# Edge rows of a 7x7 depthwise stage read out of the main operand's rows, which are reordered in DRAM

## The chip, the core and the metric

The kernel runs on one core of a Trainium2 chip. The metric is the device time of one execution in microseconds. Before the change it was 2787.28 us, the median of three runs (2781.11 to 2789.88). The profiled execution spans 2784.9 us.

## What is computed

Two layers on an image of 384 channels and 192 x 192 pixels, float32, each with a residual. The second layer is the one that the change touches: a group normalisation and a 7x7 depthwise convolution with symmetrised weights.

```python
def _L1_conv_ref(x, weight):
    w_sym = (weight + rot90(weight, 1) + rot90(weight, 2) + rot90(weight, 3)) * 0.25
    return conv(x, w_sym, stride 1, padding 3, groups=C)      # 384 x 1 x 7 x 7

# layer 0
x = x + _L0_conv_ref(_gn(x), ...)   # 1x1 to q, k, v; 2x2 max; 3x3 depthwise; channel attention; 1x1
# layer 1
x = x + _L1_conv_ref(_gn(x), L1_conv_weight)
```

## The kernel before, in words

**Three stages.** Up to about 1480 us the first layer's q and k are made and their channel attention is formed. From 1480 to about 2200 us v is made block by block, the attention is applied and projected, and the residual is added. A block is two rows of each of the six row tiles of 32 rows (`RB` = 2, `NT` = 6, `TR` = 32). From about 2210 us the 7x7 stage runs over 48 steps of eight channels (`CB` = 8).

**How the 7x7 convolution becomes matmuls.** An image row is split by column phase: `CP` = 4 phases, each with 48 columns. A partition of the operand holds one pair of row within the tile (32) and phase (4), 128 in all; its free dimension holds eight channels, six row tiles and 50 columns (`JP`, 48 and a column of padding on either side). One such run of a channel is `RUN` = 300 elements, so eight channels of a partition are 2,400 elements, or 9,600 bytes, in one piece. The operand is called `main`. A row of the output also needs rows of the tiles above and below and phases of neighbouring columns. `main` holds the 32 own rows; the three rows above and the three below lie in a second operand, `aux`, in 60 of its partitions: `HALO` = 3 rows times `NQ` = 10 column positions, from partition `TOP` = 32 and again from `BOT` = 64. The two partitions after each group of thirty hold constants: the partition `ONE` = 62 holds ones, the other three zeros. The first and last 32 partitions of `aux` are copies from `main`. For each channel there are three matmuls, two on `main` with the weights `w` and one on `aux` with the weights `h`.

**How the operands get there.** In the second stage the sums of each block stand in SBUF tiles `sx`. POOL's queue stores their rows into the DRAM buffer `sd` (L1117), whose 128 outer rows are ordered by phase, then row. For the six rows at a tile's edge it also stores them, ten column positions each and shifted by one tile, into the DRAM buffer `sh` (L1127), whose 64 outer rows are those of `aux`. The constants of `sh` are written early from a tile `z` (L629). The weights are spread out by POOL in the first stage into DRAM buffers `wt` and `wh` (`weights`, L570 to L612).

**A step of the 7x7 stage.** Before step n computes, ACT's queue issues the loads of step n+2: `w`, `h`, `main` (one transfer of 128 rows of 9,600 bytes from `sd`) and `aux` (one of 64 such rows from `sh`); all four kinds come from helpers whose transfers are recorded at line L1227. The loads of steps 0 and 1 are issued on SP's queue. There are three buffers of each. Then POOL adds the mean to the border columns of `main` and `aux` (`borders`), PE makes the sums, ACT and DVE scale them out of PSUM into `apart` (L1500, L1502), POOL gathers them into `res` (L1441), and SP's queue stores four pieces of the output per step (L1445). The order of nearly all of this is the written one: `keep` holds each instruction in the program's order on its engine. The DMA semaphores are dealt out by the framework, eight for the transfers of the SP and ACT queues, taken in turn; a transfer waits for the one that had its semaphore before.

Of the kernel before, what the change touches and what calls it, by code (L numbers as in the profile page):

```python
# [59 lines left out]
TR = 32  # L60
# [26 lines left out]
def conv_preact_d2(  # L87
# [24 lines left out]

    sd = dram.tile([CP * TR, C, RUN], F32, name="sd")

    sh = dram.tile([SHR, C, RUN], F32, name="sh")

    wt = dram.tile([P, C, 2 * P], F32, name="wt")
    wh = dram.tile([SHR, C, P], F32, name="wh")  # L120
# [442 lines left out]
    with ExitStack() as bx:  # L563
# [6 lines left out]
        def weights(kt, i0, i1):  # L570
# [30 lines left out]
            for i in range(i0, i1):  # L601
                if HALO <= i < HALO + TR:
                    continue
                f = i * NQ if i < HALO else BOT - TOP + (i - HALO - TR) * NQ
                nc.gpsimd.dma_start(
                    wh[f : f + NQ, cs].rearrange("f c n -> c f n"),
                    bass.AP(
                        g.tensor,
                        g.offset + (i - i0) * GQ * TR,
                        [g.ap[0], [TR, NQ], [1, P]],  # L610
                    ),
                )  # L612

        pieces = [
            (kt, i0, min(i0 + GR, TR + 2 * HALO))
# [3 lines left out]
        with tc.issue_after(loaded):  # L619
            for kt in range(KT):  # L620
                cs = slice(kt * P, (kt + 1) * P)
                for f in (ONE, BOT + HALO * NQ):
                    nc.sync.dma_start(
                        wh[f - TOP : f - TOP + 2, cs].rearrange("f c n -> c f n"),
                        z[:, RUN : RUN + 2 * P].rearrange("p (f n) -> p f n", f=2),
                    )
                    for k in range(2):
                        one = f + k == ONE
                        nc.sync.dma_start(  # L629
                            sh[f + k - TOP, cs], z[:, 0:RUN] if one else z[:, RUN : 2 * RUN]  # L630
                        )

# [389 lines left out]
                pin(nc.scalar.activation(gl[:, ct, h * H : (h + 1) * H], ps[:, 0:H], AF.Gelu))  # L1022
        return gl

    sdv = sd.rearrange("(v r) c n -> r c v n", v=CP)

    def dve_keep(ins):

# [33 lines left out]
    def residual(i, ot, y, xr, pin):  # L1062
# [43 lines left out]
                yield  # L1106
        cs = slice(ot * P, (ot + 1) * P)

        def rows_of(a, nv, shift):
            o = LEAD + a * RUN + shift  # L1110
            return bass.AP(
                flat.tensor, flat.offset + o, [flat.ap[0], [RB * RUN, nv], [1, RUN]]
            )

        for a in range(RB):
            r = b * RB + a
            nc.gpsimd.dma_start(sdv[r, cs], rows_of(a, CP, 0))  # L1117

            halos = []
            if r >= TR - HALO:  # L1120
                halos.append(((r - TR + HALO) * NQ, -JP))
            if r < HALO:
                halos.append((BOT - TOP + r * NQ, JP))
            for h, shift in halos:
                for q in range(0, NQ, CP):
                    nv = min(CP, NQ - q)
                    nc.gpsimd.dma_start(  # L1127
                        sh[h + q : h + q + nv, cs].rearrange("f c n -> c f n"),
                        rows_of(a, nv, shift + q // CP),
                    )  # L1130


    spare = [(NBC, ct, dy) for ct in range(KT) for dy in (1, 2)]
# [65 lines left out]
    with ExitStack() as ex_:  # L1199
# [51 lines left out]

        def load_main(n):
            main = mainbufs[n % len(mainbufs)]
            queue(n)(main.rearrange("p c t j -> p c (t j)"), sd[:, span(n)])
            return main

        def load_aux(n):
            aux = auxs[n % len(auxs)]
            queue(n)(aux.rearrange("p c t j -> p c (t j)")[TOP:REST], sh[:, span(n)])
            return aux  # L1260


# [13 lines left out]
        part = wide.tile([P, 4], F32, name="part")  # L1276
        for k, (base, q) in enumerate(((TOP, 0), (BOT, 0), (TOP, NQ - HALO), (BOT, NQ - HALO))):
            hits = ident[:, base : base + HALO * NQ].rearrange("p (h q) -> p h q", q=NQ)
            nc.vector.tensor_reduce(
                part[:, k : k + 1], hits[:, :, q : q + HALO], AX.XY, ALU.add  # L1280
            )
        nc.vector.tensor_tensor(mask[:, 3:4], part[:, 0:1], part[:, 1:2], ALU.add)
        nc.vector.tensor_tensor(mask[:, 4:5], part[:, 2:3], part[:, 3:4], ALU.add)

        mv1 = const.tile([P, KT, 2], F32, name="mv1")
        yt = const.tile([P, KT], F32, name="yt")
# [86 lines left out]
        offs = wide.tile([P, KT, P], F32, name="offs")  # L1373
        nc.vector.tensor_scalar_mul(offs[:, 0, :], ones, off1[:, 0:1])
        for n in ws:
            nc.sync.dma_start(ws[n][1][ONE : ONE + 1], offs[span(n), 0, :])
# [3 lines left out]
        nc.sync.dma_start(wh[ONE - TOP].rearrange("(t p) n -> p t n", p=P), offs)  # L1380

        def borders(n):

# [194 lines left out]
```

## Time and profile before

| what | value |
|---|---|
| median of three runs | 2787.28 us |
| span of the profiled execution | 2784.9 us |
| granted TensorE clock, mean | 0.985 |
| busy: PE, DVE, ACT, POOL | 2591.1, 2456.2, 1140.1, 746.7 us |
| bytes moved by DMA | 581.01 MB, 209 GB/s over the span |
| 7x7 stage, `main` loads of ACT's queue | 46, the first at 2213.3 us, the last at 2740.4 us |

The page cuts the span into 40 slices of some 70 us each; the 7x7 stage is the last eight of them. The row of DMA digits is the mean busy share of the core's 16 DMA engines in tenths, and GB/s is what they moved in the slice:

```profile
PE   0399999999999999999899969999999899999998
POOL 1024443100000000000111321010101478787876
DMA  9976766301010110110336997566674899999998
GB/s 381 402 252 217 249 213 228 130 34 68 35 68 35 40 62 35 68 35 0 120 103 238 340 362 231 192 230 219 203 246 151 324 343 366 372 375 372 372 374 264
```

A row such as `aux<-sh ACTq DMA_DIRECT2D x46, 600.0 KB, 10.7` in the table of DMA issues is destination and source, issuing queue, how many, the size of one, and the median time from issue to landing in us:

```profile
sd<-sx POOLq DMA_DIRECT2D x96, 600.0 KB, 10.1
out_dram<-res SPq DMA_DIRECT2D x192, 288.0 KB, 11.2
main<-sd ACTq DMA_DIRECT2D x46, 1200.0 KB, 6.7
w<-wt ACTq DMA_DIRECT2D x46, 1024.0 KB
aux<-sh ACTq DMA_DIRECT2D x46, 600.0 KB, 10.7
sh<-sx POOLq DMA_DIRECT2D x36, 600.0 KB, 16.2
h<-wh ACTq DMA_DIRECT2D x46, 256.0 KB, 3.9
sh<-sx POOLq DMA_DIRECT2D x18, 300.0 KB, 16.0
```

### The profile page before, as it was taken

How to read it: one execution, taken by the hardware profiler on the slowest of the kernel's cores; microseconds unless marked ns; L12 is line 12 of the kernel's file. 1: busy time of each engine (PE TensorE's matmuls, PEld its weight loads, DVE VectorE, ACT ScalarE, POOL GpSimd, SP SyncE). 2: the span in 40 equal slices, each digit the busy share in tenths (PEclk: the TensorE clock that was granted, in tenths of full speed). 3: DMA queues.
4: the chain of work that ended last, by engine and by line, in shares of the span. 5: the costliest groups of instructions: out<-in, count | busy, mean ns of one | idle time of the engine just before them, and what ended most of it. 6: DMA issues, size and time to landing. Idle time of an engine off the chain costs nothing. (4 is left out here: it accounts for less than half of the span.)

```text
span 2784.9 us, 25837 instructions
## 1 busy us (share of the span) xinstructions
PE 2591.1 (93%) x8365; PEld 1525.2 (55%) x8365; DVE 2456.2 (88%) x3527; ACT 1140.1 (41%) x2262; POOL 746.7 (27%) x885
## 2 busy tenths in 40 slices
PE   0399999999999999999899969999999899999998
PEld 0144444444444444444556646666666677777776
DVE  7989998989999999999789958999889789888886
ACT  0143423333343333433402312232323577777776
POOL 1024443100000000000111321010101478787876
PEclk9999999999999999999899989999999999999999
DMA  9976766301010110110336997566674899999998
GB/s 381 402 252 217 249 213 228 130 34 68 35 68 35 40 62 35 68 35 0 120 103 238 340 362 231 192 230 219 203 246 151 324 343 366 372 375 372 372 374 264
DMA packets 234039, 581.01 MB, mean 209 GB/s; under 512 B 16640, under 2 KB 165744, under 8 KB 217136
## 3 DMA queue, kind: packets, MB, share of 16 engines
q1 hardware_dynamic: 173408, 283.44, 29.0%
q0 software_dynamic: 37376, 148.85, 15.8%
q10 hardware_dynamic: 23120, 147.07, 14.1%
q8 instruction: 67, 1.10, 0.2%
q14 instruction: 68, 0.56, 0.1%
HBM read 370.93 MB, written 208.21 MB: 208 GB/s over the span
## 5 line engine op out<-in xcount | busy, mean ns | idle before, releaser
L663 PE MATMUL pq<-xq,wq 128*128 128x512 f32 x2268 | 1028.8, 597 | 5.4 <-DVE ring L673 4.7
L708 DVE SCALAR_TENSOR_TENSOR qk<-ring,wd,qk 128x384 f32<-128x384 f32 x1152 | 699.4, 616 | 59.5 <-ACT ring L695 32.1
L663 PEld LDWEIGHTS pq<-xq,wq 128*128 128x128 f32 x2268 | 408.7, 190 | 437.3 <-issue 364.0
L549 PE MATMUL pv<-xv,wq 128*128 128x384 f32 x1656 | 545.7, 490 | 26.0 <-DMA xv<-in_x_dram 21.7
L549 PEld LDWEIGHTS pv<-xv,wq 128*128 128x128 f32 x1656 | 316.7, 192 | 245.8 <-issue 20.4
L1482 PE MATMUL pc<-main,w 128*128 128x288 f32 x1536 | 436.4, 406 | 3.0 <-PE al L1515 1.7
L1502 DVE TENSOR_SCALAR apart<-pc,rb 32x576 f32<-32x576 f32 x384 | 312.1, 813 | 81.2 <-PE pc L1482 55.4
L1482 PEld LDWEIGHTS pc<-main,w 128*128 128x128 f32 x1536 | 290.6, 190 | 87.1 <-issue 2.4
L725 ACT COPY qkT<-turns 32x288 f32<-32x288 f32 x768 | 329.0, 428 | 20.7 <-DVE turns L791 9.3
L1500 ACT ACTIVATE apart<-pc,rb 32x576 f32<-32x576 f32 x384 | 281.1, 732 | 133.5 <-PE pc L1482 128.7
L959 DVE SCALAR_TENSOR_TENSOR vb<-rows,wd,vb 128x576 f32<-128x576 f32 x384 | 313.3, 817 | 11.3
L673 DVE TENSOR_REDUCE ring<-pq 128x128 f32<-128x512 f32 x428 | 292.1, 683 | 3.7 <-PE pq L663 3.6
L1482 PE MATMUL pc<-aux,h 128*128 128x288 f32 x768 | 248.1, 405 | 0.0
L719 ACT ACTIVATE junk<-qk 128x384 f32<-128x384 f32 x144 | 71.1, 494 | 411.8 <-DVE qk L708 411.0
L1441 POOL COPY res<-apart 128x1152 f32<-128x1152 f32 (+1 forms) x96 | 222.0, 2338 | 13.3 <-ACT apart L1500 9.5
L826 POOL TENSOR_TENSOR rn<-rn,halfpos 128x6 f32<-128x6 f32 x1 | 1.4, 1359 | 827.5 <-DVE rn L825 827.5
L1076 DVE TENSOR_TENSOR sx<-xr,y 128x576 f32<-128x576 f32 x180 | 203.8, 1173 | 19.9 <-ACT y L1047 14.8
L555 DVE TENSOR_REDUCE rows<-pv 128x192 f32<-128x768 f32 x144 | 137.7, 957 | 84.7 <-PE pv L549 84.6
L1117 POOL DMA_DIRECT2D sd<-sx x96 | 72.2, 755 | 514.5 <-DVE sx L1076 493.2
L741 PEld LDWEIGHTS grams<-qkT,qkT 128*96 128x96 f32 x576 | 92.8, 165 | 147.3 <-issue 136.1
L1096 ACT ACTIVATE wq<-sx,negmid 128x1152 f32<-128x1152 f32 x96 | 120.6, 1257 | 122.5 <-DVE sx L1076 118.2
L1482 PEld LDWEIGHTS pc<-aux,h 128*128 128x128 f32 x768 | 145.1, 189 | 41.2 <-issue 0.2
(227 smaller groups left out, 2270.6 us busy)
## 6 DMA issues: line engine op xcount, KB each, us to landing
sd<-sx POOLq DMA_DIRECT2D x96, 600.0 KB, 10.1
out_dram<-res SPq DMA_DIRECT2D x192, 288.0 KB, 11.2
main<-sd ACTq DMA_DIRECT2D x46, 1200.0 KB, 6.7
xv<-in_x_dram SPq DMA_DIRECT2D x138, 384.0 KB, 6.6
xr<-in_x_dram SPq DMA_DIRECT2D x45, 1152.0 KB, 11.7
xq<-in_x_dram SPq DMA_DIRECT2D x21, 2304.0 KB, 8.2
w<-wt ACTq DMA_DIRECT2D x46, 1024.0 KB
xs<-in_x_dram SPq DMA_DIRECT2D x24, 1536.0 KB, 15.1
```

The source lines that it names most:

```text
L549: nc.tensor.matmul(ps[:, u, 0 : RB * HW], wq[:, kt, o : o + P], xb[:, u, kt, :], start=(kt == 0), stop=(kt == KT - 1),)
L555: nc.vector.tensor_reduce(rows[ct][:, 1 + t0 : 1 + t0 + UT, 1 : PS + 1], ps[:, :, 0 : RB * HW].rearrange("p u (a w b) -> p u w a b", a=2, ...
L663: ins = nc.tensor.matmul(ps, wq[:, kt, ct * P : (ct + 1) * P], rows[:, kt, :, g * 64 : (g + 1) * 64], start=(kt == 0), stop=(kt == KT - 1) ...
L673: nc.vector.tensor_reduce(t[:, r0 : r0 + PR, 1 + g * 32 : 1 + (g + 1) * 32], ps.rearrange("p (h a w b) -> p h w a b", h=PR, a=2, b=2), AX. ...
L708: nc.vector.scalar_tensor_tensor(dst, src, w, dst, ALU.mult, ALU.add)
L725: nc.scalar.copy(side[f * Q : (f + 1) * Q].rearrange("p c (t n) -> p t c n", n=P)[:, :, :, a * Q : (a + 1) * Q], turns[a * Q : (a + 1) * Q ...
L959: pin(nc.vector.scalar_tensor_tensor(dst, src, w, dst, ALU.mult, ALU.add))
L1076: nc.vector.tensor_tensor(bass.AP(flat.tensor, flat.offset + at(e) + a * RUN, [flat.ap[0], [JP, NT], [1, NJ], [at(f) - at(e), 2]],), xq[:, ...
L1441: keep(copy(res[ps, k], apart[ps, :, k].rearrange("p e n -> p n e")))
L1482: nc.tensor.matmul(ahead[q][:, k, 0 : NT * NJ], lhs, rhs, start=(j == 0), stop=(j == 2), skip_group_check=True,)
L1500: keep(nc.scalar.mul(dst, src, scale))
L1502: keep(nc.vector.tensor_scalar_mul(dst, src, scale))
```

## The change

The buffer `sh` and its stores go: every edge row is already in `sd`, since a column position to the left or right of the four phases is a phase of the neighbouring column, one element on, and the tile above or below is `JP` elements before or after. `sd` is ordered by row, then phase, so that the four phases of three consecutive rows are twelve rows in a row. `aux` is loaded straight from `sd`, by two transfers for the rows above and two for the rows below: one for the first eight column positions (24 partitions) and one for the last two (6 partitions). They are issued on SP's queue. The order of the partitions within a group of thirty changes with that, and the weights `wh` and the masks follow it. The constants of `aux` are loaded once into each of the three buffers and stay there.

```diff
-    sd = dram.tile([CP * TR, C, RUN], F32, name="sd")
-    sh = dram.tile([SHR, C, RUN], F32, name="sh")
+    sd = dram.tile([TR * CP, C, RUN], F32, name="sd")
+    cst = dram.tile([3, P, RUN], F32, name="cst")
...
-                f = i * NQ if i < HALO else BOT - TOP + (i - HALO - TR) * NQ
-                nc.gpsimd.dma_start(
-                    wh[f : f + NQ, cs].rearrange("f c n -> c f n"),
...
+                base, h = (0, i) if i < HALO else (BOT - TOP, i - HALO - TR)
+                for q in range(0, NQ, CP):
+                    nq = min(CP, NQ - q)
+                    f = base + q * HALO + h * nq
+                    nc.gpsimd.dma_start(
+                        wh[f : f + nq, cs].rearrange("f c n -> c f n"),
...
-    sdv = sd.rearrange("(v r) c n -> r c v n", v=CP)
+    sdv = sd.rearrange("(r v) c n -> r c v n", v=CP)
...
         for a in range(RB):
-            r = b * RB + a
-            nc.gpsimd.dma_start(sdv[r, cs], rows_of(a, CP, 0))
-            halos = []
...
-            for h, shift in halos:
-                for q in range(0, NQ, CP):
-                    nv = min(CP, NQ - q)
-                    nc.gpsimd.dma_start(
-                        sh[h + q : h + q + nv, cs].rearrange("f c n -> c f n"),
-                        rows_of(a, nv, shift + q // CP),
-                    )
+            nc.gpsimd.dma_start(
+                sdv[b * RB + a, cs],
+                bass.AP(
+                    flat.tensor, flat.offset + LEAD + a * RUN,
+                    [flat.ap[0], [RB * RUN, CP], [1, RUN]],
+                ),
+            )
...
         def load_main(n):
             main = mainbufs[n % len(mainbufs)]
-            queue(n)(main.rearrange("p c t j -> p c (t j)"), sd[:, span(n)])
+            queue(n)(
+                main.rearrange("p c t j -> p c (t j)"),
+                bass.AP(
+                    sd.tensor, sd.offset + n * CB * RUN,
+                    [[C * RUN, CP], [CP * C * RUN, TR], [1, CB * RUN]],
+                ),
+            )
             return main
 
         def load_aux(n):
             aux = auxs[n % len(auxs)]
-            queue(n)(aux.rearrange("p c t j -> p c (t j)")[TOP:REST], sh[:, span(n)])
+            flat = aux.rearrange("p c t j -> p c (t j)")
+            for base, r, shift in ((TOP, TR - HALO, -JP), (BOT, 0, JP)):
+                for q in range(0, NQ, 2 * CP):
+                    nq = min(2 * CP, NQ - q)
+                    rows = [[1, 2], [C * RUN, HALO * CP]]
+                    if nq < 2 * CP:
+                        rows = [[CP * C * RUN, HALO], [C * RUN, nq]]
+                    rows = rows + [[1, CB * RUN]]
+                    keep(
+                        nc.sync.dma_start(
+                            flat[base + q * HALO : base + (q + nq) * HALO],
+                            bass.AP(
+                                sd.tensor,
+                                sd.offset + (r * CP * C + n * CB) * RUN + shift + q // CP,
+                                rows,
+                            ),
+                        )
+                    )
             return aux
+
+        def load_constants(aux):
+            flat = aux.rearrange("p c t j -> p c (t j)")
+            for p, k in ((ONE, 0), (BOT + HALO * NQ, 1)):
+                keep(nc.sync.dma_start(flat[p : p + 2], cst[k : k + 2, 0:CB]))
...
         hs = [load_h(n) for n in range(2)]
-        for n in range(2):
-            ws[n] = ws[n] if n == 0 else load_w(n), hs[n]
-            aux = load_aux(n)
-            mains[n] = load_main(n), aux
+        for aux in auxs[0:2]:
+            load_constants(aux)
+        mains[0] = load_main(0), load_aux(0)
+        ws[0], ws[1] = (ws[0], hs[0]), (load_w(1), hs[1])
+        main1 = load_main(1)
...
+        mains[1] = main1, load_aux(1)
+        load_constants(auxs[2])
```

In these access patterns a pair is a step in elements and a count, slowest first. Left out are the masks (`part` has six columns for six reductions where it had four), the early writes of the constants (three into `cst` where twelve went into `sh`), and `keep` around two small stores of offsets.

More of the change, by code (lines that the diff above doesn't have):

```diff
@@ L603, in weights @@
                     continue
-                f = i * NQ if i < HALO else BOT - TOP + (i - HALO - TR) * NQ
-                nc.gpsimd.dma_start(
-                    wh[f : f + NQ, cs].rearrange("f c n -> c f n"),
[L607 to L611, printed above, removed]
-                )
+                base, h = (0, i) if i < HALO else (BOT - TOP, i - HALO - TR)
[5 more added lines that the diff above has]
+                        bass.AP(
+                            g.tensor,
+                            g.offset + ((i - i0) * GQ + q) * TR,
+                            [g.ap[0], [TR, nq], [1, P]],
+                        ),
+                    )
         pieces = [
@@ L626, in conv_preact_d2 @@
                     )
[L627 to L631, printed above, removed]
+            for k in range(3):
+                nc.sync.dma_start(cst[k], z[:, 0:RUN] if k == 0 else z[:, RUN : 2 * RUN])
         ring = []
@@ L1107, in residual @@
         cs = slice(ot * P, (ot + 1) * P)
[L1109 to L1112, printed above, removed]
-            )
-        for a in range(RB):
-            r = b * RB + a
-            nc.gpsimd.dma_start(sdv[r, cs], rows_of(a, CP, 0))
-            halos = []
[L1120 to L1123, printed above, removed]
-            for h, shift in halos:
-                for q in range(0, NQ, CP):
-                    nv = min(CP, NQ - q)
-                    nc.gpsimd.dma_start(
-                        sh[h + q : h + q + nv, cs].rearrange("f c n -> c f n"),
-                        rows_of(a, nv, shift + q // CP),
-                    )
+        for a in range(RB):
+            nc.gpsimd.dma_start(
[4 more added lines that the diff above has]
+                ),
+            )
     spare = [(NBC, ct, dy) for ct in range(KT) for dy in (1, 2)]
@@ L1258, in load_aux @@
             aux = auxs[n % len(auxs)]
-            queue(n)(aux.rearrange("p c t j -> p c (t j)")[TOP:REST], sh[:, span(n)])
-            return aux
+            flat = aux.rearrange("p c t j -> p c (t j)")
[9 more added lines that the diff above has]
+                            flat[base + q * HALO : base + (q + nq) * HALO],
+                            bass.AP(
+                                sd.tensor,
+                                sd.offset + (r * CP * C + n * CB) * RUN + shift + q // CP,
+                                rows,
+                            ),
+                        )
+                    )
+            return aux
+        def load_constants(aux):
+            flat = aux.rearrange("p c t j -> p c (t j)")
+            for p, k in ((ONE, 0), (BOT + HALO * NQ, 1)):
+                keep(nc.sync.dma_start(flat[p : p + 2], cst[k : k + 2, 0:CB]))
         ws, mains = {0: load_w(0)}, {}
         hs = [load_h(n) for n in range(2)]
-        for n in range(2):
-            ws[n] = ws[n] if n == 0 else load_w(n), hs[n]
-            aux = load_aux(n)
-            mains[n] = load_main(n), aux
+        for aux in auxs[0:2]:
[3 more added lines that the diff above has]
+        main1 = load_main(1)
         mask = wide.tile([P, 5], F32, name="mask")
@@ L1275, in conv_preact_d2 @@
         nc.vector.memset(mask[0 : 2 * TR, 2:3], 1.0)
[L1276 to L1281, printed above, removed]
+        part = wide.tile([P, 6], F32, name="part")
+        for k, base in enumerate((TOP, BOT)):
+            for i, (q, nq, lo, hi) in enumerate(
+                ((0, CP, 0, HALO), (CP, CP, CP - 1, CP), (2 * CP, NQ - 2 * CP, 0, NQ - 2 * CP))
+            ):
+                o = base + q * HALO
+                hits = ident[:, o : o + nq * HALO].rearrange("p (h q) -> p h q", q=nq)
+                nc.vector.tensor_reduce(
+                    part[:, 2 * i + k : 2 * i + k + 1], hits[:, :, lo:hi], AX.XY, ALU.add
+                )
         nc.vector.tensor_tensor(mask[:, 3:4], part[:, 0:1], part[:, 1:2], ALU.add)
-        nc.vector.tensor_tensor(mask[:, 4:5], part[:, 2:3], part[:, 3:4], ALU.add)
+        nc.vector.tensor_reduce(mask[:, 4:5], part[:, 2:6], AX.X, ALU.add)
         mv1 = const.tile([P, KT, 2], F32, name="mv1")
@@ L1375, in conv_preact_d2 @@
         for n in ws:
-            nc.sync.dma_start(ws[n][1][ONE : ONE + 1], offs[span(n), 0, :])
+            keep(nc.sync.dma_start(ws[n][1][ONE : ONE + 1], offs[span(n), 0, :]))
         along(rb, rstd1, 0)()
@@ L1379, in conv_preact_d2 @@
             nc.vector.tensor_scalar_mul(offs[:, kt, :], ones, off1[:, kt : kt + 1])
-        nc.sync.dma_start(wh[ONE - TOP].rearrange("(t p) n -> p t n", p=P), offs)
+        keep(nc.sync.dma_start(wh[ONE - TOP].rearrange("(t p) n -> p t n", p=P), offs))
+        mains[1] = main1, load_aux(1)
+        load_constants(auxs[2])
         def borders(n):
```

## The prediction

> **What bounds the kernel now.** I read the table of stretches first, then the waits and the DMA table of the last stretch, because the diff changes how that stage is fed. Columns of the first fence: stretch, length, busy time of each engine, granted clock, DMA share, GB/s.
>
> ```profile
> 147.00:1480.00 1333.00, 1306.57 (x3618) 620.60 (x3617) 1218.27 (x2051) 478.04 (x1242) 171.55 (x258) 0.99 0.30 103
> 1480.00:2170.00 690.00, 658.82 (x2234) 427.80 (x2233) 599.53 (x688) 197.19 (x436) 104.63 (x140) 0.97 0.73 246
> 2170.00:2216.00 46.00, 36.63 (x145) 27.55 (x144) 29.55 (x59) 22.86 (x42) 21.59 (x34) 0.89 0.96 358
> 2400.00:2600.00 200.00, 200.00 (x826) 155.60 (x825) 172.19 (x173) 154.69 (x191) 157.52 (x155) 1.00 1.03 372
> ```
>
> Up to 2170 us PE sets the pace. In the 7x7 stage (from 2210) PE and the DMA engines are both full: share 1.03, 372 GB/s. The waits of 2216 to 2760 say which gives way:
>
> ```profile
> ACT apart L1500 <- PE pc L1482: 123.4, 47, 4.3
> POOL main L1390 <- DMA main<-sd: 78.1, 38, 3.8
> DVE apart L1502 <- PE pc L1482: 51.0, 32, 6.0
> ```
>
> The evictions wait for PE; POOL waits for `main` 38 times, 3.8 us at most. So loads arrive just in time: a transfer twice as long would stop the stage. The 45 intervals between the ACT queue's `main` loads (2213.3 to 2740.4) are 11.7 us each: that is a step. The DMA table of the same stretch gives what the rows cost:
>
> ```profile
> q10 hardware_dynamic: 20340, 143.36, 70.2%
> q1 hardware_dynamic: 72000, 53.10, 29.8%
> ```
>
> In the trace's single DMA records a 9,600-byte row (`main`, `aux`) takes 361 ns (median, 361 to 362 at the ninetieth percentile), an 8,192-byte row of `w` 309 ns, a 4,096-byte row of `h` 159 ns, a 768-byte row of `out` 36 ns. Spread over 16 engines, an engine's step is 8 rows of main (2.89 us) + 4 of aux (1.44) + 8 of w (2.47) + 4 of h (0.64) + 96 of out (3.46) = 10.9 us, against 11.7 measured. The ACT queue's share, 0.702 x 544 us = 382 us over 46.5 steps, is 8.2 us a step against 7.44 from the medians: rows of that queue took 10% more on average.
>
> [...] On the page the ACT queue has
>
> ```profile
> q10 hardware_dynamic: 23120, 147.07, 14.1%
> ```
>
> packets. Its transfers move 19,848 rows, which leaves 3,272; 205 transfers with 16 completions each would leave 3,280. Eight are missing, and just one transfer of that queue, the eight rows of `tmpr`, has fewer than 16 rows. [...]
>
> **The change, part by part.**
>
> 1. *Edge rows no longer stored.* The 54 stores `sh<-sx` (36 x 600 + 18 x 300 KB = 27.6 MB) go. At 372 GB/s these are 74 us of all engines, and they fall between 1489 and 1680, where the DMA share is 0.85 to 1.03. PE waits there:
>
> ```profile
> PE pv L549 <- DMA xv<-in_x_dram: 21.7, 3, 15.9
> ```
>
> Without these stores that stretch moves what the next one does (share 0.63 to 0.68, no such wait), so I count **-22 us**, -10 if half is another transfer's doing.
>
> 2. *54 stores of `wh` instead of 18*: 36 more issues on POOL at 0.95 us (`wh<-g`, L605), 34 us, mostly before 520 us, where POOL's digits on the page are 2 to 4 and it waits 189 us itself for `wt<-g` and `wh<-g`. No wait list of that stretch names POOL as a releaser that holds PE. 0. Six edge constants of 300 KB in all become three: 0. The six `part` reductions instead of four (0.15 us each on DVE) and the new order of SP's first loads: 0 and under 1 us.
>
> 3. *`sd` rows by (row, phase) instead of (phase, row).* The 96 stores have the same 512 rows of 1,200 bytes; only the step between them changes. 0. The load of `main` changes shape: the source is now 4 phases x 32 rows x 9,600 bytes, the destination 128 partitions. [...]32 rows on each of engines 0 to 3 instead of 8 on each of 16. 32 x 0.361 = **11.55 us** on those four.
>
> 4. *Edge rows of `aux` from `sd`, on SP.* 60 rows instead of 64, by two transfers with source 2 x 12 rows and destination 24 partitions ([...]12 rows each on engines 0 and 1) and two with source 3 x 2 and destination 6 ([...]2 rows each on 0 to 2). Engine 0: 2 x 12 + 2 x 2 = 28 rows, **10.1 us**, instead of 4 rows.
>
> Engine 0's step is then 11.55 + 10.1 + 2.47 + 0.64 + 3.46 = **28.2 us**, with eleven completions 28.4. If the rows of main, aux, w and h take the 10% more that the ACT queue's did, 30.9. [...] I take 29.5. PE's 48 matmuls, DVE's and POOL's work of a step fit in 11.7 us and lie beside it. The loads run up to two steps ahead into three buffers, so engine 0 has a queue; each interval grows by 29.5 - 11.7 = 17.8 us, and 47 intervals by **+837**.
>
> 5. *Start of the stage.* `main` of step 0 is issued at 2193.7 and POOL takes it at 2203.7. With 11.55 + 10.1 = 21.7 us on engine 0 and about 2 us of completion it is 2217: **+12**, since aux now queues beside it. The chain of the normalisation (to 2209) hides none of what lies beyond.
>
> 6. *A new wait.* In the changed program's order a step has 11 transfers on SP and ACT where it had 8, and each waits for the completion of the one eight places earlier: SP's second edge transfer waits for `main` of the step before, and behind it in SP's queue stand the other two and four stores; ACT's `main` load waits for a store of the step before, and behind it stand ACT's evictions, for which PE's sums wait. All of these are shorter than engine 0's own queue, so I price it at 0; at the most two completions a step are exposed, 2 x 2.8 us (the shortest landing of `out`).
>
> Sum: 2787 - 22 + 12 + 837 = **3614 us**.
>
> **The rivals.**
>
> - *All 16 engines work whatever the pattern* (faster). For: main and aux carry the same bytes in rows of the same 9,600 bytes, and POOL's transfers with mixed shapes fill all engines now. Against: those have 128 on both sides, and the missing eight completions show that row counts matter on the hardware queues. Aux is 4 rows fewer, the stage stays at PE's 11.7, part 1 remains: 2787 - 22 = 2765. Chance 0.09.
> - *The narrow transfers lie on different engines.* Main on four, aux on others: 11.55 + 2.47 + 0.64 + 3.46 = 18.1, with 5% 19.0; 47 x 7.3 = 343; 2787 - 22 + 6 + 343 = 3114. [...] Chance 0.06.
> - *Part 6 is exposed*: 29.5 + 5.6 = 35.1 a step; 47 x 23.4 = 1100; 3877. For: eight counters for eleven transfers, and SP already waits 198.9 us for earlier stores. Against: there are two queues, and a transfer of the other keeps engine 0 busy. Chance 0.13.
> - *Engine 0 bounds, near its own sum* (the forecast): 28.4 to 30.9, so 3562 to 3680. Chance 0.72.
>
> **How the numbers follow.** The time is the forecast's. Range: the forecast's bounds, with a gain of 10 instead of 22 and a start of up to 20 late above, and half-exposed completions (32.3 a step, 3746): 3530 to 3780. That leaves out the two cheap rivals (0.15) and the worse half of the third. Slower by over 0.3% are the last three cases, 0.91; faster 0.07; 0.02 within 0.3%, where all engines work and the gain of part 1 is made elsewhere.
>
> **What would show it.** Part 3 and 4: on the page after, the ACT queue has 23,120 - 46 x 80 (aux with completions) - 46 x 12 (completions of main) = 18,888 packets; 19,440 if main uses 16. The DMA digits of the last stage fall from 9 to about 4, PE's too, and 372 GB/s to some 150; POOL waits for `main` or `aux` some 18 us a step; `main` lands 12 us or more after issue, instead of 6.7. Part 1: no wait of PE for `xv` near 1640. Wrong, if the stage still takes 11.7 us a step: then the engine count doesn't follow the outer dimension. If the step is above 33 us with engine 0 not full, part 6 failed.

## The result, and the profile after

The changed kernel takes 3817.66 us, the median of four runs (3796.8 to 3841.02). The kernel before takes 2786.57 us, the median of four (2781.11 to 2789.88). The ratio is 1.3706, with a 95% interval of 1.3651 to 1.3761. The forecast was 3614 us, with a range up to 3780: the direction and the main mechanism were right, the size was too small by 204 us. The profiled executions span 2784.9 us before and 3825.3 us after; all stages below are compared in these two.

The slices of the page of after, PE's and the DMA engines' busy tenths and what was moved:

```profile
PE   0799999999999899999999643252352433523425
DMA  9766631111111044666665634444444444444444
GB/s 390 291 242 231 227 116 46 50 50 50 50 50 50 1 136 163 215 224 226 226 225 177 214 103 141 118 126 120 117 136 119 115 134 127 127 125 117 134 114 130
```

The 7x7 stage now fills seventeen slices of 96 us where it filled eight of 70. In it the DMA engines are busy four tenths of the time and move 103 to 141 GB/s; before it was nine tenths and 372. PE, full before, works two to five tenths. Nothing is full on average: a mean over sixteen engines can hide that a few of them have most of the work. In the single DMA records at most four rows of any kind are under way in 63% of the time (2400 to 3600).

The page's table of DMA queues, ACT's and SP's:

```profile
q1 hardware_dynamic: 175312, 308.59, 24.4%
q10 hardware_dynamic: 18888, 118.80, 11.0%
```

18,888 packets on ACT's queue is what the prediction worked out for a `main` load on four engines. Had it kept sixteen, there would be 46 x 12 = 552 more completions. The single DMA records agree: from 2400 to 3600 ACT's queue never has more than four rows of 9,600 bytes under way at once, but for 0.3% of the time; before, it had up to sixteen. SP's queue has no more than three under way but for 0.04% of the time, and both queues together no more than four but for 0.7%, which fits edge rows on engines that carry `main`; the records don't name engines.

Two stretches of after, columns as in the prediction's first fence:

```profile
1620.00:1690.00 70.00, 70.00 (x242) 45.79 (x241) 64.29 (x72) 22.39 (x50) 7.50 (x10) 1.00 0.60 197
2400.00:2600.00 200.00, 77.81 (x288) 58.58 (x288) 49.77 (x60) 53.99 (x66) 53.75 (x54) 0.69 0.45 122
```

And the first of them before:

```profile
1620.00:1690.00 70.00, 48.30 (x146) 28.98 (x145) 39.36 (x45) 11.42 (x25) 14.11 (x19) 0.80 0.94 321
```

From 1620 to 1690 PE had stood still for 22 us, waiting for `xv` under a DMA share of 0.94. After, it is full. The last addition into `sx` starts at 2162.0 us instead of 2194.9: a gain of 33 us by the end of that stage. From 2400 to 2600 PE is busy 78 of 200 us, where it was busy all 200.

The waits of 2400 to 3600 in after, first of the compute engines, then of SP's queue:

```profile
POOL aux L1437 <- DMA aux<-sd: 907.6, 54, 45.6
ACT apart L1527 <- PE pc L1509: 865.1, 34, 52.7
PE pc L1509 <- POOL aux L1444: 777.1, 18, 47.5
```

```profile
SPq L1265 <- DMA main<-sd: 344.3, 17, 21.8
SPq L1472 <- DMA aux<-sd: 219.2, 53, 11.2
SPq L1472 <- DMA w<-wt: 200.1, 17, 13.5
SPq L1472 <- DMA out_dram<-res: 125.9, 18, 9.0
```

Read from below: PE waits for POOL, POOL waits for the rows of `aux` to land. SP's queue, which issues these rows (L1265), is itself held 17 times until a `main` has landed: that is the wait for a semaphore which part 6 of the prediction named and priced at nothing. The instructions of `main` in after, ACT's loads alone (duration of the issue in ns as lowest, median and highest, then first and last start):

```profile
L1213 ACTq DMA_DIRECT2D main<-sd x46: 579/580/630, 2218.0 to 3753.5; - x46
```

(3753.5 - 2218.0) / 45 = **34.1 us** a step, against 11.7 before and 29.5 forecast. The account of the whole: 33 us earlier into the stage; the first of these loads 37.6 us later after the stage's beginning (4.7 us later on the clock); 45 intervals of 22.4 us more, 1008.4; and 27.3 us more after the last load. -32.9 + 37.6 + 1008.4 + 27.3 = 1040.4, the difference of the spans (it must come out, since the four are cut from the same two spans).

### The profile page after: what moved, and what is told of

It is laid out like the page before. It is cut to its first block, busy times and chain, and to the rows that moved or that the text cites. A ratio compares the mean times of both kernels' runs of the same rounds, so it can differ in the third digit from the quotient of the medians.

```text
span 3825.3 us, 26098 instructions
## 1 busy us (share of the span) xinstructions
PE 2651.4 (69%) x8365; PEld 1560.4 (41%) x8365; DVE 2367.0 (62%) x3529; ACT 1140.7 (30%) x2262; POOL 715.7 (19%) x867
## 3 DMA queue, kind: packets, MB, share of 16 engines
q1 hardware_dynamic: 175312, 308.59, 24.4%
q10 hardware_dynamic: 18888, 118.80, 11.0%
## 5 line engine op out<-in xcount | busy, mean ns | idle before, releaser
L1509 PE MATMUL pc<-aux,h 128*128 128x288 f32 x768 | 278.7, 448 | 987.7 <-POOL aux L1444 940.3
L1509 PEld LDWEIGHTS pc<-aux,h 128*128 128x128 f32 x768 | 157.0, 209 | 1045.2 <-POOL aux L1444 976.8
L1509 PE MATMUL pc<-main,w 128*128 128x288 f32 x1536 | 473.6, 434 | 19.5 <-POOL main L1417 13.1
L1509 PEld LDWEIGHTS pc<-main,w 128*128 128x128 f32 x1536 | 316.1, 206 | 118.4 <-POOL main L1417 16.5
L1437 POOL TENSOR_TENSOR aux<-aux,mm 32x96 f32<-32x96 f32 x96 | 41.9, 436 | 1139.2 <-DMA aux<-sd 1137.5
L1076 DVE TENSOR_TENSOR sx<-xr,y 128x576 f32<-128x576 f32 x180 | 203.9, 1174 | 19.4 <-ACT y L1047 15.2
L1468 POOL COPY res<-apart 128x1152 f32<-128x1152 f32 (+1 forms) x96 | 207.5, 2192 | 5.8 <-DVE apart L1529 3.0
```

What stands on the lines that cost most here:

```text
L1076: nc.vector.tensor_tensor(bass.AP(flat.tensor, flat.offset + at(e) + a * RUN, [flat.ap[0], [JP, NT], [1, NJ], [at(f) - at(e), 2]],), xq[:, ...
L1468: keep(copy(res[ps, k], apart[ps, :, k].rearrange("p e n -> p n e")))
L1509: nc.tensor.matmul(ahead[q][:, k, 0 : NT * NJ], lhs, rhs, start=(j == 0), stop=(j == 2), skip_group_check=True,)
```

## The experiments

All experiments are read by that step, and beside it stands the sum of the rows on engine 0. By that name the prediction has the engine with a share of every load; no record names one, so the sum is an estimate, from the counts of engines and the durations that the prediction took from the trace of before (9,600-byte row 361 ns, `w` 309, `h` 159, `out` 36). "Wide" is a load whose larger part lies on twelve or sixteen engines, "narrow" one on two to four. The four runs of the changed kernel differ by up to 44 us, which is 1 us a step; all experiments but two were run once, and several on different chips, so differences of a step under 1 us are not read.

| kernel | `main` | `aux` | transfers a step | rows of engine 0, us | step, us | excess |
|---|---|---|---|---|---|---|
| before | wide | wide | 8 | 10.9 | 11.7 | 0.8 |
| both_wide_eight | wide | wide | 8 | 10.9 | 11.9 | 1.0 |
| after_both_wide | wide | wide | 11 | 11.6 | 14.5 | 2.9 |
| after_main_wide | wide | narrow | 11 | 19.6 | 20.9 | 1.3 |
| main_four | narrow | wide | 8 | 19.6 | 26.4 | 6.8 |
| after_aux_wide | narrow | wide | 11 | 20.3 | 27.6 | 7.3 |
| main_four_aux_two | narrow | narrow | 8 | 29.7 | 32.2 | 2.5 |
| after | narrow | narrow | 11 | 28.2 | 34.1 | 5.9 |

### Is it the number of engines?

Only `main` narrow, in the kernel before (`sh` and its stores stay):

```diff
-    sdv = sd.rearrange("(v r) c n -> r c v n", v=CP)
+    sdv = sd.rearrange("(r v) c n -> r c v n", v=CP)
...
-            queue(n)(main.rearrange("p c t j -> p c (t j)"), sd[:, span(n)])
+            queue(n)(
+                main.rearrange("p c t j -> p c (t j)"),
+                bass.AP(sd.tensor, sd.offset + n * CB * RUN,
+                    [[C * RUN, CP], [CP * C * RUN, TR], [1, CB * RUN]]),
+            )
```

> The kernel before with one part of the change alone: rows of sd ordered by row and phase, and main loaded as 4 x 32 rows. sh, its stores and the single aux transfer stay, eight transfers a step. Theory N (narrow transfers: [...]the fullest engine's rows are the step): 11.55 + 1.44 + 2.47 + 0.64 + 3.46 = 19.6 us a step nominally, 20 to 21 measured, 3180 to 3230 us in all. Theory W (the new waits of eleven transfers made the step, width costs nothing): 11.7 us a step, 2787 us. Theory H (a narrow transfer also holds up what stands behind it, in both queues, so a step is 1.2 times the fullest engine's rows as in the changed kernel, 34.1 to 28.2): 23.7 us, 3350 us.

3485.94 us, where the kernel before took 2781.46 on that chip; 26.4 us a step, (3426.9 - 2239.4) / 45 by the first and last start in its loads of `main`:

```profile
L1227 ACTq DMA_DIRECT2D main<-sd x46: 579/580/958, 2239.4 to 3426.9; - x46
```

ACT's queue has 22,568 packets, 552 fewer than before: twelve completions fewer for each of the 46 loads. So the width of one load costs 700 us with no transfer, byte or wait added, and the theory that the pattern doesn't matter falls. But the step isn't the 20 to 21 us of engine 0's rows either. Its waits of 2400 to 3400, compute engines and SP's queue:

```profile
POOL res L1447 <- DMA out_dram<-res: 545.5, 22, 34.6
```

```profile
SPq L1451 <- DMA out_dram<-res: 816.8, 99, 20.6
```

The stores of the output, which no compute engine waited for in this stage before, hold POOL's `res` and through it DVE.

The same with the 64 rows of `aux` read as 2 x 32 from `sh`, so that they lie on two engines:

```diff
-            queue(n)(aux.rearrange("p c t j -> p c (t j)")[TOP:REST], sh[:, span(n)])
...
+                bass.AP(sh.tensor, sh.offset + n * CB * RUN,
+                    [[C * RUN, 2], [2 * C * RUN, SHR // 2], [1, CB * RUN]]),
```

> As the run before, and aux as one transfer of 2 x 32 rows from sh, so on two engines; it reads the rows in another order, which changes what is computed. Eight transfers a step and ACT's queue as before. Theory N: engine 0 has 32 + 32 rows: 11.55 + 11.55 + 6.57 = 29.7 us, 30 to 31 measured, 3650 to 3700 us. Theory W: 11.7 us, 2787 us. Theory H: 1.2 x 29.7 = 35.6 us, about 3910 us.

3784.84 us; 32.2 us a step, for 29.7 us of rows. ACT's queue has 21,924 packets, 46 x 14 fewer than with `main` alone narrow, so two engines for `aux` instead of sixteen. Two narrow loads, with eight transfers and SP's queue left to the stores, already give almost the changed kernel's time.

The changed kernel with `main` read wide, 128 rows in their order:

```diff
-                bass.AP(sd.tensor, sd.offset + n * CB * RUN,
-                    [[C * RUN, CP], [CP * C * RUN, TR], [1, CB * RUN]]),
+            queue(n)(main.rearrange("p c t j -> p c (t j)"), sd[:, span(n)])
```

> The changed kernel with main read as 128 rows one after the other (in the wrong order of rows, which changes what is computed); aux narrow on SP, eleven transfers a step. Theory N: 2.89 + 10.1 + 6.57 = 19.6 us a step, 20 to 21 measured, 3150 to 3190 us with the 33 us that the stage before it gained. Theory W: the waits are the same, so 34 us a step and 3800 us. Theory H: 23.5 us, 3310 us.

3197.34 us; 20.9 us a step, which is engine 0's sum of 19.6 and a little. ACT's queue has 19,440 packets, the count for sixteen engines.

The changed kernel with `aux` read as 24 and 6 rows in one piece each, which go on twelve and six engines:

```diff
-                    rows = [[1, 2], [C * RUN, HALO * CP]]
-                    if nq < 2 * CP:
-                        rows = [[CP * C * RUN, HALO], [C * RUN, nq]]
+                    rows = [[C * RUN, nq * HALO]]
...
```

> The changed kernel with the edge rows read as 24 and as 6 rows one after the other (other rows than the right ones, which changes what is computed), so on 12 and 6 engines; main narrow, eleven transfers a step. Theory N: 11.55 + 6 rows 2.17 + 6.57 = 20.3 us a step, 20.5 to 21.5 measured, 3170 to 3220 us. Theory W: 34 us a step, 3800 us. Theory H: 24.4 us, 3350 us.

3534.57 us; 27.6 us a step for 20.3 us of rows. Both narrow patterns cost, and the kernels with both of them, 32.2 and 34.1 us, lie above each alone, 20.9 and 26.4, as they must if the same engines carry both. SP's queue of the changed kernel has 175,312 packets against 176,560 here, 1,248 fewer: in 48 steps two edge transfers with ten completions fewer and two with three fewer, so two and three engines instead of twelve and six. Where `main` is narrow and `aux` wide there is a large excess.

### What do eleven transfers cost?

Both of the last two edits together:

> The changed kernel with main read as 128, the edge rows as 24 and 6 rows one after the other (the rows are not the right ones, which changes what is computed): 16, 12 and 6 engines, while the eleven transfers a step, their queues and the waits between them stay. Narrow transfers as the cause: the fullest engine has 8 + 6 rows of 9,600 bytes, 5.05 + 6.57 = 11.6 us; 11.7 to 12.3 us a step, 2750 to 2790 us. Waits of the eleven transfers as the cause of the part above engine 0's rows (34.1 - 28.2 = 5.9 us): 17 us a step, 3000 us.

2887.06 us; 14.5 us a step. Between the two theories: without narrow loads nearly 3 us above the 11.6 us of rows are left. SP's waits of 2300 to 2800:

```profile
SPq L1464 <- DMA w<-wt: 245.0, 35, 9.3
SPq L1257 <- DMA main<-sd: 65.8, 34, 3.3
```

Stores (L1464) wait for `w` loads of ACT's queue, with which they have nothing to do but the semaphore. If that is the cost, the same kernel with eight transfers should lose it. `aux` as one load of 64 rows from `sd`, still on SP's queue:

```diff
...
+            keep(nc.sync.dma_start(flat[TOP:REST], sd[TOP:REST, span(n)]))
```

> As the run of the changed kernel with both wide (14.5 us a step), but aux is one transfer of 64 rows of sd on SP's queue, so eight transfers a step instead of eleven (other rows than the right ones, which changes what is computed). If the number of transfers over the eight semaphores makes the 2.8 us: 11.7 us a step, 2755 us. If it is aux standing on SP's queue among the stores: 14 to 14.5 us, 2880 us.

2762.51 us; 11.9 us a step. Its SP waits of 2300 to 2700:

```profile
SPq L1449 <- DMA out_dram<-res: 93.4, 75, 4.5
SPq L1449 <- DMA w<-wt: 12.9, 3, 7.3
```

The wait for `w` falls from 35 times in 500 us to 3 in 400. Three transfers more a step cost **2.6 us**, 14.5 - 11.9, where all loads are wide. In it is the wait that the prediction described and priced at 0, but not that wait alone: engine 0 has six rows of `aux` in the first and four in the second, and a row of `aux` took 522 ns on average in the first (2300 to 2800) and 387 in the second (2300 to 2700). By these means, taken for engine 0 too, the rows are an estimated 1.6 us of the 2.6. Nor is 2.6 us a fixed price: the changed kernel with `main` wide has eleven transfers too, and lies 1.3 us above its rows.

### What is the rest of the excess?

The output stores cut to one of the twelve rows of each partition, so 8 instead of 96 small rows on an engine, as many transfers as ever; first with `main` narrow in the kernel before, then in the changed kernel:

```diff
-                        out[c : c + 2].rearrange("c (t r) w -> r (c t) w", t=NT),
+                        out[c : c + 2].rearrange("c (t r) w -> r (c t) w", t=NT)[:, 0:1],
```

> The kernel with main on four engines alone (sh kept, eight transfers a step, 26.4 us a step where the fullest engine's rows are 19.6 us), each of the four stores of a step cut to one of its twelve rows per partition, so most of the output isn't written: transfers and waits as before, 8 instead of 96 rows of 768 bytes on an engine. Theory S ([...]the stores take longest and POOL's res buffers are held): the fullest engine's rows are 16.4 us; 16.5 to 18 us a step. Theory C (main waits for the main before it to have landed, and the gap of completion, issue and first row is the 6.8 us): 26.4 - 3.2 = 23.2 us.

20.55 us a step instead of 26.4 (3175.04 us).

> The changed kernel with each store of the 7x7 stage cut to one of twelve rows per partition, so most of the output isn't written; transfers and waits stay. Fullest engine 28.2 - 3.2 = 25.0 us. Theory S[...]: 25 to 27 us a step, 3380 to 3480 us. Theory C (waits for completions among the eleven transfers): 34.1 - 3.2 = 31 us, 3670 us.

28.65 us a step instead of 34.1 (3570.24 us). Both lie between the theories: 3.2 us of rows less saved 5.9 and 5.5 us. Why more is saved than the rows took isn't shown. And 4 us of excess stay. In the records of the first of these kernels from 2400 to 3000 the 9,600-byte rows take 361 ns (median of 2,193) while no row of `w` or `h` moves, and 658 ns (1,260 rows) while eight or more of those move. So the next theory was that rows collide. It was tried on four kernels by loading, from step 3 on, only 16 partitions of `w` and `h`:

```diff
-            queue(n)(w, wt[:, span(n)])
+            m = P if n < 3 else 16
+            queue(n)(w[0:m], wt[0:m, span(n)])
```

> Main alone on four engines, as in the run of that name (26.4 us a step, rows of engine 0 19.6), and from step 3 on w and h are loaded for 16 of their 128 and 64 partitions only, one row on each engine (the rest of their weights is left as it was, so the sums are other ones). Transfers and waits stay as many. Engine 0's rows: main 11.55 + aux 1.44 + w 0.31 + h 0.16 + out 3.46 = 16.9 us. Theory C (main's rows are slow only beside rows of w and h, and that makes the excess): 16.9 to 18.5 us a step. Theory L (the excess belongs to the narrow transfer and stays): 26.4 - 2.6 = 23.8.

20.9 us a step (3233.57 us): between, 4.0 us above the rows.

> The changed kernel with w and h loaded for 16 partitions only from step 3 on (the rest of their weights is left as it was). Engine 0's rows: 28.2 - 2.6 = 25.6 us, and 2.6 for eleven transfers. Theory C: 28.2 us a step. Theory L: 34.1 - 2.6 = 31.5.

29.3 us a step (3601.04 us): between, nearer to the collision.

> Main on four engines, output stores cut to one row of twelve (20.55 us a step before, engine 0's rows 16.4), and in addition w and h loaded for 16 partitions only from step 3 on (the rest of weights and output is left out). Rows: 13.75 us. Theory C: 13.8 to 14.8 us a step. Theory L: 20.55 - 2.6 = 17.9. The row records should show nearly all rows of main at 361 ns if C holds.

23.5 us a step (3341.78 us): **neither**. It moves less than the kernel with long weights (20.55 us), and is slower; its 9,600-byte rows, with hardly anything else moving, took 617 ns on average from 2300 to 3100. Collision with `w` and `h` can't be the main cause. (The kernel with long weights ran on another chip, where the kernel before takes 2760 us instead of 2786.) The timeline of its ACT queue and engine:

```profile
2420.19 0.58 ACTq L1227 DMA_DIRECT2D main<-sd  x1
2421.44 0.52 ACTq L1227 DMA_DIRECT2D aux<-sh  x1
...
2442.78 0.59 ACTq L1227 DMA_DIRECT2D main<-sd  x1
2444.05 0.52 ACTq L1227 DMA_DIRECT2D aux<-sh  x1
2444.62 0.73 ACT L1508 ACTIVATE apart<-pc,rb 32x576 f32<-32x576 f32 x1 [13.46 <-DMA aux<-sh]
```

ACT stands still for 13.46 us behind the two issues, until the `aux` of the step before has landed. Eight transfers a step on eight semaphores taken in turn mean that each load gets the semaphore of the load of its own kind of the step before, and isn't issued until that one has landed. (In the trace of before each of the four kinds has one semaphore from ACT's second load on, in all 45.) There are three buffers, but one load of each kind under way.

That wait is there, but it need not be what makes the step long. In the DMA records of this kernel from 2400 to 3000, four rows or more are under way in over 88% of the time, and none in 0.3%: the engines of `main` aren't left without rows. Engine 0's 36 rows of 9,600 bytes, at the mean of 617 ns, are 22.2 us of the 23.5. ACT waits long because the rows are long.

> The changed kernel with stores cut to one row of twelve (28.65 us a step before) and w and h loaded for 16 partitions only from step 3 on (the rest of weights and output is left out). Rows: 22.4 us, and 2.6 for eleven transfers. Theory C: 25.0 us a step. Theory L: 28.65 - 2.6 = 26.0. These lie near each other; it shows mainly whether the sum of rows and 2.6 is reached once little else moves.

25.05 us a step (3408.32 us). That is what the first theory's sum gave, 22.4 us of rows and 2.6 for eleven transfers, but the two theories lie only 1 us apart, and the run before this one, with as little else to move, is 10 us above its rows. So it decides nothing, and the agreement may be luck.

The last theory that was tested was the depth that the semaphores leave. The four stores go to POOL's queue, which has semaphores of its own (in the traces of before and after, eight for POOL's transfers and eight others for those of SP and ACT); the rows stay:

```diff
-                    nc.sync.dma_start(
+                    nc.gpsimd.dma_start(
                         out[c : c + 2].rearrange("c (t r) w -> r (c t) w", t=NT),
```

> Main alone on four engines (26.4 us a step, rows of engine 0 19.6), with the four stores of a step on POOL's queue: four transfers a step remain on SP and ACT, so that a load waits for one of two steps before, and two steps of loads can lie with engine 0. Rows are the same. Theory D (the depth that the semaphores leave makes the excess): 19.6 to 21 us a step. Theory R (rows of narrow transfers are slower by themselves): 26 or more. If POOL's queue itself becomes the bound, its four issues and its copies would show it busy throughout.

21.9 us a step instead of 26.4 (3294.1 us): of 6.8 us of excess 2.3 are left, a little above what that theory said and far from its rival. The loads of `main`:

```profile
L1227 ACTq DMA_DIRECT2D main<-sd x46: 579/579/630, 2240.5 to 3224.4; - x46
```

> The changed kernel (34.1 us a step, rows 28.2) with the four stores of a step on POOL's queue: seven transfers a step remain on SP and ACT. Theory D: the 2.6 us of the eleven transfers go and the rest of the excess too, 28.2 to 29.5 us a step. Theory R: only the 2.6 us go, 31.5.

30.1 us a step instead of 34.1 (3642.46 us): of 5.9 us of excess 1.9 are left, between the two theories and nearer to the depth. With seven transfers a step, SP's queue still waits for `main` (2400 to 3100):

```profile
SPq L1265 <- DMA main<-sd: 567.3, 22, 27.6
```

So most of the excess goes when the stores leave the eight semaphores. This edit also puts the stores' rows into another queue, and the 9,600-byte rows of ACT's queue became shorter with it: mean 406 ns instead of 514 in the changed kernel, 2300 to 3100. On engine 0's 32 rows of `main` that is 3.5 of the 4.0 us. The runs don't separate the two causes, but the records bound the depth. Depth can only close gaps, stretches in which an engine has no row under way. With `main` narrow, fewer than four rows are under way in 6.1% of the time (2400 to 3000), 1.6 us a step, and in 0.8% with the stores on POOL: at most about 1.5 of the 4.5 us gained. In the changed kernel no row is under way in 2% of the time, and a single one in another 2%.

What then are the 5.9 us of excess in the changed kernel? From 2400 to 3600 the rows of `main` take 517 ns on average and those of `aux` 392. With 32 and 28 of them on engine 0, and 6.6 us for the other rows at their durations of before, the sum is 16.5 + 11.0 + 6.6 = **34.1 us**, the measured step. It is an estimate, and its meeting the step to the tenth is luck, since the means are over all engines with such rows (the rows of the output grew too, from 36 to 52 ns on average). But it leaves little room for gaps: engine 0 had a queue, and its rows were longer.

### Is it enough to keep sixteen engines?

Two kernels give `main` sixteen engines by another pattern. The kernel before, with the 128 partitions read as 16 x 8 rows of `sd`:

```diff
+                    [[C * RUN, 4 * CP], [4 * CP * C * RUN, 8], [1, CB * RUN]],
```

> The kernel before, with main alone read in another form: 16 x 8 rows of sd (other rows than the right ones in their places, which changes what is computed), still on 16 engines, 8 rows each, one transfer, eight transfers a step. [...] Width and number of transfers as causes: no change, 11.7 us a step, 2787 us. Theory P, after the main rows of 704 ns in the run with rows in 16 and 12: [...]a row of main takes twice as long: 8 x 0.361 = 2.9 us more on every engine, 10.9 + 2.9 = 13.8 us, 14 to 15 us a step, 2890 to 2940 us.

2925.67 us, 2760.63 before on that chip; 15.2 us a step, (2872.0 - 2188.3) / 45:

```profile
L1227 ACTq DMA_DIRECT2D main<-sd x46: 553/578/1662, 2188.3 to 2872.0; - x46
```

The same width (23,120 packets on ACT's queue, as before), number of transfers and bytes, and 3.5 us more. The 9,600-byte rows took 638 ns in the median instead of 361. Theory P's row, 2 x 361 = 722 ns, is not far off, but it was an estimate after the 704 ns of the next run. What lengthens the rows isn't shown: the edit changes which row of `sd` goes to which partition, and no run takes apart what follows from that.

Then the changed kernel with `sd` ordered so that all edges can be read in patterns of 12 rows and `main` in 16 x 8, with 13 transfers a step:

```diff
...
-    sdv = sd.rearrange("(r v) c n -> r c v n", v=CP)
+    sdv = sd.rearrange("(b v a) c n -> b a c v n", b=8, v=CP)
...
+                    rows = [[4 * C * RUN, HALO * CP]]
+                    if nq < CP:
+                        rows = [[4 * CP * C * RUN, HALO], [4 * C * RUN, nq]]
```

> The change's idea with patterns that keep their engines: sd ordered by row within eight, then phase, then eighth of the tile, so that main is 16 x 8 rows (16 engines) and a group of twelve edge rows is 12 rows at one step (12 engines); the last two column positions stay 3 x 2 rows (3 engines). Thirteen transfers a step. Rows of the fullest engine: 8 + 8 rows of 9,600 bytes 5.78 + 6.57 = 12.35 us. Width alone: 12.4 to 12.8 us a step, 35 to 50 us above before, less the 0 to 33 us of the stores left out. With the price of more transfers than semaphores as in the run with both wide (2.8 us for eleven): 15.2 to 16 us a step, 2900 to 2950 us.

3180.3 us; 20.7 us a step, worse than expected, with 19,440 packets on ACT's queue, so `main` on sixteen engines: its rows of 9,600 bytes on ACT's queue, those of `main`, took 704 ns in the median. This version of the idea leaves no part out, and it is still 14% above the kernel before.

### What are the edge stores worth?

The kernel before without the 54 stores into `sh`:

```diff
...
-            queue(n)(aux.rearrange("p c t j -> p c (t j)")[TOP:REST], sh[:, span(n)])
+            queue(n)(aux.rearrange("p c t j -> p c (t j)")[TOP:REST], sd[TOP:REST, span(n)])
```

> The kernel before without the 54 stores of edge rows; aux is loaded as 64 rows of sd, which leaves the right edge rows out. What the missing stores are worth alone. If the trace's shift of the stage's end in the changed kernel (33 us) is theirs: 2753 us. If only PE's wait for xv is (21.7 us): 2765 us. If a transfer other than these stores held xv up: 2787 us.

2758.88 us in 20 runs, and 2760.45 in 23 of the kernel before on the same chip: ratio 0.9992 (0.9981 to 1.0004). Nothing. On this chip the kernel before is 27 us faster than on the first, and with all edge stores in place (the run with `main` narrow and short stores, on the same chip) the stretch reads

```profile
1620.00:1690.00 70.00, 69.76 (x240) 44.90 (x239) 62.81 (x70) 23.74 (x52) 14.13 (x19) 1.00 0.95 347
```

The DMA share is as high as before, 0.95, yet PE doesn't wait. So the stall that part 1 removes is there on some chips and not on others. The other runs that keep the edge stores agree: PE's wait for `xv` is 22 to 25 us on the three more chips where the kernel before takes 2778 to 2786 us, and 3.0 us on one where it takes 2761. Each chip was used at one time only, so chip and occasion can't be told apart. In the run with eight transfers, on a chip where the kernel before takes 2788.05 us, the stores are gone and 2762.51 was measured, 25.5 us less; that is one run.

Last, the edges left in `sh`, but copied there out of `sd` by 60 transfers within DRAM on POOL's queue, instead of being stored from `sx`:

```diff
+            nc.gpsimd.dma_start(
+                sh[f].rearrange("(a b) n -> a (b n)", b=CB),
+                bass.AP(sd.tensor, sd.offset + row * C * RUN + shift,
+                    [[CB * RUN, C // CB], [1, CB * RUN]]),
+            )
```

> A version meant to beat both: the kernel before, its loads and its order of sd unchanged, but the edge rows of sh are filled by 60 copies from sd to sh in DRAM (48 pieces of 9,600 bytes each, three after each block's stores from the sixth block on), in the stretch after 1690 us where the DMA share is 0.65, instead of 54 stores between 1489 and 1680. If the burst of stores holds xv up on this chip (before near 2785 us): 25 to 33 us less. If it doesn't (before near 2760 us, as on the chip of the last runs): no difference, or up to 10 us more if the copies hold up a load of xv or xr in their turn.

2755.43 us in 6 runs, 2788.05 in 11 of the kernel before: ratio 0.9893 (0.9867 to 0.9919). It is 1.1% faster than the kernel before on this chip; the changed kernel, 37% slower on the first, wasn't run there. The copies were issued from 1506.9 to 1753.5 us, earlier than expected, and they do no harm to the stretch:

```profile
1620.00:1690.00 70.00, 70.00 (x242) 45.78 (x241) 63.72 (x71) 23.75 (x52) 13.57 (x22) 1.00 0.92 307
```

The share is 0.92, nearly that of before, but PE stays full; why this traffic doesn't hold up `xv` and the stores did isn't shown. The loads of `main` and `aux` stay wide, and the step is 11.7 us. On a chip without the stall such a gain isn't shown.

## Why the prediction was wrong in size

- **Parts 3 and 4, the engines** (right): `main` on four engines, the edge rows on two and three. These counts were the author's estimate, which the trace of before couldn't show; after, the packets agree with them (18,888, and 1,248 fewer on SP's queue than with wide edge loads). Which engines they are isn't shown, since the traces don't name them, but the steps and the rows of both loads together, over four under way in only 0.7% of the time, agree with shared ones. The rivals with all engines at work or on different engines are refuted: 20.9 us a step with narrow `aux` alone, 26.4 with `main` alone, 32.2 to 34.1 with both.
- **"Part 6 ... I price it at 0"** (wrong where all loads are wide, open here): the argument was that these waits are shorter than engine 0's own queue. Eleven instead of eight transfers cost 2.6 us a step with everything wide, longer rows among them. In the changed kernel SP's queue does wait for `main`, but at most one row was under way in only 4% of the time, 1.4 us a step, so little of the step seems to be such a wait laid bare. (The records don't name the engine, so this is no strict bound.)
- **"The loads run up to two steps ahead into three buffers, so engine 0 has a queue"** (wrong in the reason, right in what follows): the buffers allow it, the eight semaphores don't. With eight transfers a step each load waits for the one of its kind of the step before (13.46 us of ACT in the step shown above). Rows were under way nearly throughout all the same: none in 0.3% of the time there, and in 2% in the changed kernel. Stores off these semaphores brought 4.0 us a step in the changed kernel and 4.5 in that with narrow `main`, but most of that is in shorter rows.
- **Engine 0's step, 29.5 us** (mis-sized; this is the step of the prediction that failed): 34.1, which over 45 intervals is 207 of the 213 us that the spans grew beyond the forecast. The count of rows was right; their length was wrong. The forecast took 361 ns for a row of 9,600 bytes and put 10% on the rows of `main`, `aux`, `w` and `h`, a figure from wide loads. Rows of `main` took 517 ns on average and those of `aux` 392, and with these the sum is some 34 us. What lengthens a narrow load's rows stays open: collision with `w` and `h` was expected to be enough, and wasn't; moving the stores to another queue brought `main` to 406 ns, but doesn't say why.
- **Start and intervals**: the forecast had +12 at the start and 47 intervals; 45 were read off, with 37.6 before and 27.3 after them, 65 in all where 12 + 2 x 17.8 = 48 stood. The 2 us of completion in the +12 are an estimate; the trace of before has an `out` store land 2.8 us after issue at the shortest, of which its 24 rows on an engine are 24 x 36 ns = 0.9.
- **Part 1, -22 us** (right in kind): 33 here, some 25 on one other chip, and none on a third, on which the wait for `xv` isn't there.
- **Parts 2 and the new order of `sd`, 0**: nothing in the first stage or in the 96 stores contradicts it.

The rival "Part 6 is exposed" had 35.1 us a step and 3877 us and came nearest, but by luck: it added 5.6 us of bare waits to 29.5, and the records show longer rows instead. The test that the prediction set itself was a step above 33 us with engine 0 not full. The first half came true, the second is not borne out.

## What to carry to other kernels

Find out for every load how many engines carry its pattern before merging or reordering rows in DRAM: the packets of its queue and the rows under way at once show it (here 128 rows in order had up to sixteen under way, and 4 x 32 rows four, with twelve packets fewer a load). Then add up the rows of the fullest engine: that sum was a floor for the step in every kernel here, and a mean DMA share of 0.45 can hide it. Don't take a row's duration over from a wide load to a narrow one (361 ns and 517 here); read it from a run. Then count the transfers of a step against the semaphores they share: three buffers gave no depth that the eight semaphores took away, and a load waited for the one of its kind of the step before. If the aim is to unburden a stretch of stores, move them to another source or queue and leave the shape of the loads alone, as the version with copies within DRAM did.

## What was not expected of the hardware

- The number of engines isn't all: on sixteen engines, `main` read as 16 x 8 took 15.2 us a step instead of 11.7, with rows of 638 ns in the median instead of 361.
- Rows of a load on four engines can take 617 ns on average with hardly any other traffic (main on four engines, short stores and weights), and 361 in the median in a quiet stretch of another kernel. No run here explains both.
- The same kernel takes 2760 us on some chips and 2787 on others, and the difference of 27 us is near the wait for `xv` under the burst of stores, 22 to 25 us.
